# Narrow products for norms and key sums in a decoder layer's cross-attention, with ScalarE in written order

## The chip, the core and the metric

The kernel runs on one core of one Trainium2 chip. The metric is the device time of one execution in microseconds (us); lower is better. The core has TensorE (PE; its weight loads are listed as PEld), VectorE (DVE), ScalarE (ACT), GpSimd (POOL) and SyncE (SP, which here only issues DMAs), each with an instruction stream of its own, kept in step by semaphores.

## The reference

One decoder layer in float32 over x of shape (16, 128, 1024), three blocks with residuals:

```python
x = x + attn(layernorm(x), Wqkv, bqkv, Wo, bo)                 # 256 wide, one head
x = x + xattn(layernorm(x), ctx, ctx, Wq, Wk, Wv, Wo, bo, g)   # linear attention
x = x + ffn(layernorm(x), gate, up, down)                      # int4 weights, 1024 -> 2752 -> 1024
```

The second block takes each batch as 128 channels by 1024 positions. That is the one that the change is about:

```python
qh = softmax(Wq @ q, axis=-2) * SCALE   # 8 heads of 64, over the 64 channels of a head
kh = softmax(Wk @ k, axis=-1)           # over the 1024 positions
context = einsum('bhdn,bhen->bhde', kh, vh)
out = einsum('bhde,bhdn->bhen', context, qh) ; out = Wo @ out + bo
norm = maximum(sqrt(sum(out * out, axis=1)), 1e-12)   # over the 128 channels
return out / norm * g * sqrt(128)
```

Two sums over partitions occur in it: the denominators of the key softmax (per key channel, over positions) and the norm (per position, over the 128 channels).

## The kernel before

The program holds the layer twice: a fast form that takes exponentials without subtracting a maximum and raises a flag where a sum leaves a safe range, and a second form behind a branch, which runs only then. All that follows is about the fast form.

Stage 1 is self-attention over four groups of four batches, up to about 250 us. Beside it `early`, a generator made by `prepare`, dequantises int4 weights on VectorE (`pa`, then combinations `pc`) and stores them to DRAM as `wg`, `wu` and so on.

Stage 2 is cross-attention, from about 250 to 750 us, one batch after the other in the order of `batches`. The loop over a batch `b` alternates four times `key_unit` (for the next batch) and `query_unit` (for this one), and calls `tick()` after each, so a batch is eight units. Everything else is put in a list by `later(n, fn)`, "n ticks from now". TensorE, VectorE and SP are wrapped in `InOrder`, which keeps the instructions in the order in which the code emits them; ScalarE's and GpSimd's are placed by the scheduler.

- `key_unit`: a projection into a PSUM pair `kq` (two buffers), one exponential of 1024 columns on ScalarE into `ek`, and two units later a product with the context, `kx`. VectorE adds the four `ek` of a batch into `ksum`; at the end it adds its two halves.
- `mix`: four products of one column each with `ones` give the key sums (`mm<-ones,ksum`); then eight products of 64 output rows (`mm<-g_sb,kc`), which VectorE scales into `m_sb`.
- `query_unit`: a projection into `kq`, an exponential into `qe`, sums and reciprocals on VectorE, a multiplication on GpSimd, a transposing on VectorE (`kt`), and a trip through DRAM (`kd`, then `qs`, both issued by SP).
- `project_out(b, qs, st, when)`: four pieces of the output product at the ticks `when[0..3]`; ScalarE makes `y` and its square `sq` from each half. `norms`, at `when[4]`, multiplies `sq` by a 128 x 128 `ones`, so that all 128 output rows hold the same sums; ScalarE takes the logarithm and then exp(-0.5 ln) of [128, 1024], each with a load of its table. `scale`, `add`, `stats`, `row_shift` and `turned` follow one tick apart; `turned` normalises the row for stage 3 into `xn`, and `turn_rows` transposes it and stores it as `xt`.
- `rows` normalises the next batch's row on ScalarE (`xn`), after a small `row_shift` on VectorE.

`when` is written out by hand, for most batches:

```python
when = (14, 15, 16, 17, 18, 1, 1) if k < 13 else (13, 14, 15, 16, 17, 1, 1)
```

Stage 3 is the gated feed-forward block, by two levels of a seven-product scheme (`GATE`, `DOWN`). `one_block` multiplies the rows with weight tiles `w`, which `load_weights` brings from DRAM; `got` adds a PSUM bank and a kept copy into `sg` (gate) or `h` (up). `beside` runs between products; it ticks until the leftovers of stage 2 are done, calls `attention_done`, which makes the generator `rest` for the weights not yet prepared, and then takes steps of `rest`. VectorE and SP keep the written order here too. Stage 4, from about 1740 us, is the down projection.

Most helpers go through `InOrder`, so that their instructions all carry line 63 in the profile, and are told apart by their tiles.

Of the kernel before, what the change touches and what calls it, by code (L numbers as in the profile page):

```python
# [18 lines left out]
P = 128  # L19
# [47 lines left out]
def decoder_layer(  # L67
# [83 lines left out]
    def normalise_act(dst, src, b):  # L151
        nc.scalar.activation(
            dst, src, AF.Identity, bias=shift[:, b : b + 1], scale=rstd[:, b : b + 1]
        )
# [50 lines left out]
    def prepare(jobs, ahead, queue, vector=nc.vector, sync=nc.sync):  # L205
# [4 lines left out]
        stores = deque()  # L210

# [101 lines left out]
    give_pool = ExitStack()  # L313
    ag = give_pool.enter_context(tc.tile_pool(name="a_g", bufs=1, reuse_waits="tile"))
    with (
# [31 lines left out]
        def turn(b, xnT):  # L347

            xn = a2.tile([P, C], F32, name="xn")
            normalise(xn, X[b], b)  # L350
            nc.vector.tensor_copy(*turn_half(xn, xnT, b, 0))
            nc.scalar.copy(*turn_half(xn, xnT, b, 1))

        def first_rows(xnT):

            vector = InOrder(tc, nc.vector)
            halves = {}

            def stats(b):
                row_stats(b, vector)  # L360
                row_rstd(b, 1, vector)

            def rows(b):
                xn = a2.tile([P, C], F32, name="xn")
                row_shift(b, vector)
                normalise_act(xn, X[b], b)
                halves[b] = turn_half(xn, xnT, b, 0)
                nc.scalar.copy(*turn_half(xn, xnT, b, 1))

            def copy(b):  # L370
                vector.tensor_copy(*halves[b])

            for fn, b in (
                (stats, 0),
                (stats, 1),
                (rows, 0),
                (rows, 1),
                (stats, 2),
                (copy, 0),
                (copy, 1),  # L380
                (stats, 3),
                (rows, 2),
                (rows, 3),
                (copy, 2),
                (copy, 3),
            ):
                fn(b)
# [74 lines left out]
        def attend(atT, v):  # L462
            oT = ag.tile([P, 2, TB], F32, name="oT")
            for d in range(2):
                ps = aps.tile([P, BPT, S], F32, name="mm")
                for i in range(BPT):
                    nc.tensor.matmul(
                        ps[:, i, :], v[:, i, ts(d, P)], atT[:, i, :], start=True, stop=True
                    )
                nc.scalar.copy(oT[:, d, :], ps.rearrange("p i s -> p (i s)"))  # L470
            return oT
# [10 lines left out]
        for t in range(NT):  # L482
# [27 lines left out]
            v = a2.tile([P, BPT, DH], F32, name="v")  # L510
# [26 lines left out]
    sync = InOrder(tc, nc.sync)  # L537
# [66 lines left out]
    bek = unit_pool("b_ek", 3)  # L604
# [33 lines left out]
    if True:  # L638
# [17 lines left out]
        nc.sync.dma_start(wk_sb, xwk)  # L656
        ctxs = {batches[0]: load_ctx(batches[0])}
        wo_again = []
        for d in range(2):
            wo_again.append(bqs.tile([P, C], F32, name="wo_again", tag="qs"))  # L660
            nc.sync.dma_start(wo_again[d], wo[ts(d, P)])
        nc.sync.dma_start(wq_sb, xwq)
        nc.sync.dma_start(wv_sb, xwv.rearrange("(r p) s -> p r s", p=P))
        nc.sync.dma_start(xwo_sb, xwo.rearrange("(r p) o -> p r o", p=P))
        nc.sync.dma_start(xbo_sb, xbo)
        nc.sync.dma_start(gs_sb, xg)
        ctxs[batches[1]] = load_ctx(batches[1])
# [9 lines left out]
        def raise_flag():  # L677

            within = [bsm.tile([P, 1], F32, name=f"within{n}") for n in range(2)]

            def test(n):
                op, limit, holds = (
                    (ALU.max, LIMIT, ALU.is_le),
                    (ALU.min, 1 / LIMIT, ALU.is_ge),
                )[n]
                vector.tensor_reduce(within[n], sums, AX.X, op)
                vector.tensor_scalar(within[n], within[n], limit, None, holds)

            def count():
                ps = bps.tile([P, 1], F32, name="mm")  # L690
                for n in range(2):
                    tensor.matmul(ps, ones, within[n], start=(n == 0), stop=(n == 1))
                vector.tensor_copy(flag, ps[0:1])

            later(1, lambda: test(0))
            later(2, lambda: test(1))
            later(5, count)

        def mix_weights():

            D = DIM_HEAD
            for e in range(2):
                ps = bps.tile([P, 4, S], F32, name="mm")
                for r in range(4):
                    tensor.matmul(
                        ps[:, r, :],
                        wv_sb[ts(e, D), r, :],
                        xwo_sb[ts(e, D), r, :],
                        start=True,
                        stop=True,  # L710
                    )
                dst = g_sb.rearrange("p (r e) o -> p e r o", e=2)[:, e]
                nc.scalar.mul(dst, ps, D**-0.5)
# [15 lines left out]
        def key_unit(ctx, p, st):  # L729
# [14 lines left out]
            ek = bek.tile([P, 2, 512], F32, name="ek")  # L744
            nc.scalar.activation(ek, ps, AF.Exp)

            def use():
# [11 lines left out]
                if p == 1:  # L759
                    st["sum"] = bas.tile([P, 2, 512], F32, name="ksum")  # L760
# [3 lines left out]
                if p == 3:  # L764
                    t = st["sum"]
                    vector.tensor_tensor(t[:, 0], t[:, 0], t[:, 1], ALU.add)
                    st["kc"] = b1.tile([P, HIDDEN], F32, name="kc")
                    nc.scalar.copy(st["kc"], st["ps"])
                    later(4, lambda: mix(st))
# [3 lines left out]
        def mix(st):  # L773

            D = DIM_HEAD
            ks = bps.tile([P, 4], F32, name="mm")
            for r in range(4):
                tensor.matmul(
                    ks[:, r : r + 1], st["sum"][:, 0, ts(r, P)], ones[:, 0:1], start=True, stop=True
                )  # L780
            ksum = sums_tile(4, B * 8 * HEADS + 4 * st["b"], "ksum")
            krec = bsm.tile([P, 4], F32, name="krec")
            vector.tensor_copy(ksum, ks)
# [18 lines left out]
        def query_unit(b, pair, qs, wait):  # L802
# [9 lines left out]
            if plain:  # L812
                nc.scalar.activation(qe, heads, AF.Exp)  # L813
            else:
# [3 lines left out]
                nc.scalar.activation(qe, qe, AF.Exp)  # L818
# [31 lines left out]
        def turned(b):  # L850

            xn = b1.tile([P, 2 * JC, P], F32, name="xn3")
            for n in range(2):
# [3 lines left out]
                normalise_act(dst, rows, b)  # L857
# [8 lines left out]
        def project_out(b, qs, st, when):  # L866
            out, bank = {}, {}

            def piece(h, part):
                if h == part == 0:  # L870
                    out["y"] = b1.tile([P, C], F32, name="y")
                    out["sq"] = b1.tile([P, C], F32, name="sq")
                if part == 0:
                    bank[h] = bps.tile([P, 512], F32, name="mm")
                ps, y, sq = bank[h], out["y"], out["sq"]
# [10 lines left out]
                nc.scalar.activation(y[:, ts(h, 512)], ps, AF.Identity, bias=xbo_sb)  # L886
                nc.scalar.activation(sq[:, ts(h, 512)], ps, AF.Square, bias=xbo_sb)

            def norms():
                y, sq = out["y"], out["sq"]  # L890

                for h in range(2):
                    ps = bps.tile([P, 512], F32, name="mm")
                    tensor.matmul(ps, ones, sq[:, ts(h, 512)], start=True, stop=True)
                    nc.scalar.activation(sq[:, ts(h, 512)], ps, AF.Ln)
                nc.scalar.activation(sq, sq, AF.Exp, scale=-0.5)
                steps = (scale, add, stats, lambda: row_shift(b, vector), lambda: turned(b))
                for n, step in enumerate(steps):
                    later(when[5] + n * when[6], step)
# [16 lines left out]
        def rows(b):  # L916
            xn = b0.tile([P, C], F32, name="xn2", tag="xn2")
            row_shift(b, vector)
            normalise_act(xn, X[b], b)
            return xn  # L920

        T0 = {}

# [18 lines left out]

        xns = {batches[0]: rows(batches[0])}
# [10 lines left out]
        for k, b in enumerate(batches):  # L954
# [4 lines left out]
            if len(ahead) == 2:  # L959
                when = (14, 15, 16, 17, 18, 1, 1) if k < 13 else (13, 14, 15, 16, 17, 1, 1)  # L960
            elif ahead:
                when = (12, 13, 14, 15, 16, 1, 0)
            else:
                when = (10, 10, 11, 11, 12, 1, 1)
            project_out(b, qs, keys[b], when)
            if ahead:
                later(5, lambda n=ahead[0]: xns.update({n: rows(n)}))
            if len(ahead) == 2:
                later(2, lambda n=ahead[1]: ctxs.update({n: load_ctx(n, sync)}))
            for n in (5,) if k < 12 else ():  # L970
# [11 lines left out]
    give_pool.close()  # L982
# [57 lines left out]
    with ExitStack() as gs:  # L1040
# [4 lines left out]
        cw = pool("c_w", 5)  # L1045
# [4 lines left out]
        def attention_done():  # L1050
# [6 lines left out]
            rest = prepare(todo[MIDDLE:], 2, nc.sync, vector)  # L1057
# [28 lines left out]
        def load_weights(queue=nc.sync):  # L1086
            if to_load:
                wt = cw.tile([P, 2, 512], F32, name="w")
                todo = to_load.popleft()
                for n, (blk, mat, q) in enumerate(todo):  # L1090
# [480 lines left out]
        for n in range(AHEAD):  # L1571

            load_weights(nc.scalar if n == 0 else nc.sync)
# [5 lines left out]
        def beside(n, mat, q):  # L1579
# [19 lines left out]
            if rest is None or blk == 0:  # L1599
                return  # L1600
            if blk == RB:
# [3 lines left out]
            else:  # L1605
                more = mat == "g" and blk < 4
                steps = (1, 1 + (mat == "g"), 1, more, 1, 0, 0)[n % 7]
# [310 lines left out]
```

## Time and profile before

| | |
|---|---|
| time, three runs | 2221.77, 2221.79, 2223.6 us (median 2221.79) |
| the profiled execution | 2223.65 us, its span 2221.8 us |
| TensorE busy | 2191.3 us, 99% of the span |
| VectorE, ScalarE, GpSimd busy | 1559.9, 507.7, 562.6 us |
| DMA | 425.27 MB, mean 191 GB/s |
| granted TensorE clock over the span | 0.997 |

Times in the profile are counted from the span's start. A group of instructions is shown as line, engine, operation, output<-inputs, shapes and count, and then its busy time, the mean of one in ns, and the idle time of the engine before it with what ended it. A matrix product in float32 appears as two records. The ends of products are modelled, so that the start of the next one tells more than a duration.

### The profile page before, as it was taken

To read this page: it belongs to the slowest core of one execution; us is meant where nothing else is said; L and a number is where in the kernel's file an instruction comes from. 1 tells how busy PE (TensorE), PEld (TensorE's weight loads), DVE (VectorE), ACT (ScalarE), POOL (GpSimd) and SP (SyncE) were. 2 spreads that over 40 slices of the span, in tenths; PEclk is the share of its full clock that TensorE was granted. 3 is DMA by queue.
4 is the path that set the end of the run, shared out by engine and by line. 5 is a ranking of instruction groups with operands and counts; after the bars stand their busy time and mean duration, and the time that the engine had idled before them with its cause. 6 is when DMAs were issued, how large, how long until landed. Compare 5 with 4: busy or idle time off the path is not lost.

```text
span 2221.8 us, 24458 instructions
## 1 busy us (share of the span) xinstructions
PE 2191.3 (99%) x8500; PEld 1547.4 (70%) x8500; DVE 1559.9 (70%) x2119; ACT 507.7 (23%) x684; POOL 562.6 (25%) x442
## 2 busy tenths in 40 slices
PE   8999999999999998999999999999999999999998
PEld 7556555555555553444788588888887788888887
DVE  7897577888887647675799768787786645544462
ACT  2111235665556531111111111212121000000000
POOL 5453134333333300000344244444442000000000
PEclk9999999999999999999999999999999999999999
DMA  6435447777795758999434735464455965334631
GB/s 253 159 127 188 138 147 239 225 233 230 231 294 183 237 176 279 286 327 283 161 115 139 202 102 180 143 209 164 159 199 184 342 198 184 102 120 140 218 119 40
DMA packets 268725, 425.27 MB, mean 191 GB/s; under 512 B 28784, under 2 KB 130544, under 8 KB 268464
## 3 DMA queue, kind: packets, MB, share of 16 engines
q1 hardware_dynamic: 239584, 368.54, 52.3%
q0 software_dynamic: 10704, 35.92, 4.4%
q10 hardware_dynamic: 18304, 19.14, 2.7%
q8 instruction: 70, 1.15, 0.2%
q14 instruction: 63, 0.52, 0.1%
HBM read 265.62 MB, written 157.35 MB: 190 GB/s over the span
## 4 chain that ended last, share of the span: by engine, by line
PE 91%; DVE 5%; issue 2%; DMA 1%; SPq 0%; ACT 0%; POOL 0%; DVEq 0%; POOLq 0%; ACTq 0%
PE q L63 24%; PE po L1797 21%; PE p L63 13%; PE kq L63 10%; PE mm L63 8%; PE kx L63 5%; PE mm L397 4%; PE p L1166 2%; PE mm L412 2%; DVE pa L63 2%; PE mm L295 1%; DVE ti L63 1%; DVE C L63 1%; PE tr L344 1%; DVE pc L63 0%
## 5 line engine op out<-in xcount | busy, mean ns | idle before, releaser
L63 PE MATMUL q<-ti,li 128*128 128x256 f32 x1176 | 271.6, 380 | 3.6 <-ACT k L63 3.3
L63 PEld LDWEIGHTS q<-ti,li 128*128 128x128 f32 x1176 | 222.5, 190 | 37.7 <-POOL li L63 5.2
L63 POOL TENSOR_TENSOR li<-w 128x512 f32<-128x512 f32 x98 | 141.2, 1443 | 340.1 <-DMA w<-wu 293.5
L63 PE MATMUL p<-b,w 128*128 128x512 f32 x432 | 192.6, 598 | 6.4 <-DVE sg L63 6.4
L825 POOL TENSOR_TENSOR qe<-qe,qrec 128x1024 f32<-128x1024 f32 x64 | 148.1, 2314 | 180.1 <-DVE qrec L63 156.0
L63 ACT COPY k<-q 128x512 f32<-128x512 f32 x147 | 85.9, 584 | 464.9 <-PE q L63 464.9
L1797 PE MATMUL po<-wc,lc 128*128 128x256 f32 x840 | 183.4, 379 | 0.0
L1797 PEld LDWEIGHTS po<-wc,lc 128*128 128x128 f32 x840 | 159.6, 190 | 21.8
L63 PEld LDWEIGHTS p<-b,w 128*128 128x128 f32 x432 | 82.7, 192 | 110.9 <-issue 99.9
L63 PE MATMUL p<-T,w 128*128 128x512 f32 x304 | 134.7, 592 | 0.0
L1797 PE MATMUL po<-wq,lq 128*128 128x256 f32 x560 | 126.7, 379 | 0.4 <-issue 0.4
L63 PEld LDWEIGHTS mm<-qs,m_sb 128*128 128x128 f32 x512 | 97.3, 190 | 40.1 <-issue 29.7
L63 DVE STREAM_TRANSPOSE kt<-qe 128x1024 f32<-128x1024 f32 x64 | 79.4, 1241 | 64.5 <-POOL qe L825 62.3
L63 PE MATMUL kq<-wq_sb,xn 128*128 128x512 f32 x256 | 120.3, 593 | 1.6 <-ACT qe L813 1.6
L63 PE MATMUL kx<-ek,cxt 128*128 128x512 f32 x256 | 121.8, 598 | 0.0
L63 PE MATMUL mm<-qs,m_sb 128*128 128x256 f32 x512 | 120.8, 379 | 0.0
L63 PE MATMUL kq<-wk_sb,cx 128*128 128x512 f32 x256 | 120.1, 592 | 0.0
L1797 PEld LDWEIGHTS po<-wq,lq 128*128 128x128 f32 x560 | 106.0, 190 | 16.1 <-issue 1.3
L397 PE MATMUL mm<-xnT,wqkv_sb 128*128 128x512 f32 (+1 forms) x320 | 113.3, 510 | 0.0
L63 POOL TENSOR_TENSOR li<-w,li 128x512 f32<-128x512 f32 x49 | 66.2, 1352 | 180.1 <-PE q L63 179.6
L63 DVE TENSOR_TENSOR pa<-pa,sz 128x1024 f32<-128x1024 int32 x86 | 108.8, 1265 | 2.4
L63 PEld LDWEIGHTS p<-T,w 128*128 128x128 f32 x304 | 57.8, 190 | 72.7 <-issue 72.2
(193 smaller groups left out, 3755.6 us busy)
## 6 DMA issues: line engine op xcount, KB each, us to landing
w<-wu SPq DMA_DIRECT2D x140, 256.0 KB, 3.4
lq<-h SPq DMA_DIRECT2D x140, 256.0 KB, 4.4
w<-wg SPq DMA_DIRECT2D x138, 256.0 KB, 2.8
kd<-kt SPq DMA_DIRECT2D x64, 512.0 KB, 3.6
qs<-kd SPq DMA_DIRECT2D x256, 128.0 KB, 3.3
h<-hc SPq DMA_DIRECT2D x80, 256.0 KB, 2.8
wq<-wd SPq DMA_DIRECT2D x70, 256.0 KB, 5.2
h<-h SPq DMA_DIRECT2D x60, 256.0 KB, 2.1
```

The source lines that it names most:

```text
L63: return lambda *args, **kw: self._tc.keep_in_program_order(fn(*args, **kw))
L295: tensor.matmul(ps, oT[:, d, ts(b % BPT, S)], wo_d[d][:, ts(h, 512)], start=(d == 0), stop=(d == 1),)
L344: nc.tensor.transpose(tr[:, j, :], xn[:, ts(4 * h + j, P)], ident)
L397: nc.tensor.matmul(ps[:, tokens], wqkv_sb[:, f, c, :], xnT[:, c, tokens], start=(c == 0), stop=(c == CC - 1),)
L412: nc.tensor.matmul(ps, xnT[:, c, ts(i, S)], wqkv_sb[:, 4:6, c, :], start=(c == 0), stop=(c == CC - 1),)
L825: nc.gpsimd.tensor_tensor(qe, qe, rec.unsqueeze(2).to_broadcast(wide), ALU.mult)
L1166: tensor.matmul(ps, wt[:, j, :], T[q][:, :, j], start=(first == q and j == 0), stop=(q in (2, 3, 4) and j == JC - 1), skip_group_check=True,)
L1797: nc.tensor.matmul(bank[:, i, :], l[:, ts(i, S)], w,  start=(start and c == 0 and i % 2 == 0), stop=(stop and c == len(pairs) - 1), skip_g ...
```

## The change

1. `norms`, for the batches k = 0 to 12: four products with `ones[:, :32]`, each for 256 positions, write to partitions 0, 32, 64 and 96 of one [128, 256] tile. The logarithm and the exponential are 256 columns wide. The four rows go to a small DRAM tensor `rn_flat` by ScalarE's DMA queue, and one unit later the same queue loads them back, broadcast to all 128 partitions of `sq`. The last three batches keep the direct form (`direct_norm`).
2. `mix`: the key sums come from eight products of 32 output rows and 128 columns, accumulated over the two halves of `ksum`, and a transposing on VectorE; the addition of the halves goes away.
3. ScalarE is wrapped in `InOrder` in stage 2. `row_shift` is emitted two units before `rows`; the steps after `norms` are spaced 3, 4, 5, 7 and 9 ticks from it, and two pieces of the output product come one tick earlier. The squares are made before `y`.
4. The tiles `oT`, `xn`, `v` of stage 1, `ek` and `ksum` of stage 2 and `w` of stage 3 share one pool of five buffers; the first weight tile of stage 3 is loaded a batch ahead, on SP. The loads at the start of stage 2 go through the ordered SP.
5. The first step of `rest` only issues its loads, and the steps beside the products of stage 3 are dealt out anew.

```diff
-        def project_out(b, qs, st, when):
+        def project_out(b, qs, st, when, direct_norm):
...
-                for h in range(2):
-                    ps = bps.tile([P, 512], F32, name="mm")
-                    tensor.matmul(ps, ones, sq[:, ts(h, 512)], start=True, stop=True)
-                    nc.scalar.activation(sq[:, ts(h, 512)], ps, AF.Ln)
-                nc.scalar.activation(sq, sq, AF.Exp, scale=-0.5)
+                if direct_norm:
...
+                else:
+                    ps = bps.tile([P, 2 * P], F32, name="mm")
+                    for c in range(4):
+                        tensor.matmul(
+                            ps[ts(c, Q)], ones[:, :Q], sq[:, ts(c, 2 * P)], start=True, stop=True
+                        )
+                    rn = sq[:, ds(0, 2 * P)]
+                    scalar.activation(rn, ps, AF.Ln)
+                    scalar.activation(rn, rn, AF.Exp, scale=-0.5)
+                    flat = dram.tile([4, 2 * P], F32, name="rn_flat", tag="rn_flat", bufs=2)
+                    scalar.dma_start(flat, rn[0:P:Q])
+                    row = flat.rearrange("c n -> (c n)").partition_broadcast(P)
+                    later(1, lambda: scalar.dma_start(sq, row))
...
-            if len(ahead) == 2:
-                when = (14, 15, 16, 17, 18, 1, 1) if k < 13 else (13, 14, 15, 16, 17, 1, 1)
...
+            if k < 12:
+                when = (14, 15, 15, 16, 18, (3, 4, 5, 7, 9))
+            elif k == 12:
+                when = (14, 15, 15, 16, 17, (3, 4, 5, 6, 8))
...
-            for r in range(4):
-                tensor.matmul(
-                    ks[:, r : r + 1], st["sum"][:, 0, ts(r, P)], ones[:, 0:1], start=True, stop=True
-                )
...
+            ks = bps.tile([P, 4, Q], F32, name="mm")
+            parts = st["sum"].rearrange("p i (r c q) -> p i c r q", r=4, c=4)
+            for i in range(2):
+                for c in range(4):
+                    tensor.matmul(
+                        ks[ts(c, Q)], ones[:, :Q], parts[:, i, c], start=(i == 0), stop=(i == 1)
+                    )
+            kt = st["sum"][:, 0, ds(0, P)]
+            vector.transpose(kt, ks.rearrange("p r q -> p (r q)"))
...
-            rest = prepare(todo[MIDDLE:], 2, nc.sync, vector)
+            rest = prepare(todo[MIDDLE:], 2, nc.sync, vector, loads_first=True)
...
-                more = mat == "g" and blk < 4
-                steps = (1, 1 + (mat == "g"), 1, more, 1, 0, 0)[n % 7]
+                steps = (1, 1 + (n == 1 < blk), 1, n == 3 and blk < 4, 1, 0, 0)[n % 7]
```

## The prediction

> **What bounds the kernel now.** I read the page first, then the list of waits for TensorE, TensorE's groups with shapes kept apart, the table of stages, and the timelines round three places.
>
> ```profile
> span 2221.8 us, 24458 instructions
> PE 2191.3 (99%) x8500; PEld 1547.4 (70%) x8500; DVE 1559.9 (70%) x2119; ACT 507.7 (23%) x684; POOL 562.6 (25%) x442
> ```
>
> TensorE is idle for 30.5 us of the span. So a gain has two sources only: less time in its products, or less of that idle time. The waits say which engine ends the latter:
>
> ```profile
> PE tr L344 <- ACT xn L152: 9.2, 1, 9.2
> PE p L63 <- DVE sg L63: 6.4, 2, 6.1
> PE kq L63 <- ACT qe L813: 1.6, 1, 1.6
> ```
>
> The first is the start of the program, which the change leaves. The groups that it touches, with two for comparison (count, busy us, mean ns):
>
> ```profile
> L63 PE MATMUL mm<-sq,ones 128*128 128x512 f32 x64 | 30.2, 592 | 0.0
> L63 PE MATMUL mm<-ones,ksum 128*128 128x1 f32 x128 | 15.2, 240 | 0.0
> L63 PE MATMUL mm<-g_sb,kc 128*64 128x128 f32 x256 | 17.5, 279 | 0.0
> L427 PE MATMUL mm<-qkT 128*128 128x128 f32 x64 | 7.8, 275 | 0.0
> ```
>
> Two records stand for one float32 product (64 records of `sq`, 32 products in the code). The mean is a latency; the busy time divided by the count is the spacing. A 128-column product on the whole array takes 7.8 / 64 = 0.122 us a record; one with 64 output rows (`g_sb,kc`, "128*64") takes 17.5 / 256 = 0.068. Two products on the two halves of the array therefore run side by side. Inside one batch:
>
> ```profile
> 342.08 0.95 PE L63 MATMUL mm<-ones,ksum 128*128 128x1 f32 x8
> 342.96 1.09 PE L63 MATMUL mm<-g_sb,kc 128*64 128x128 f32 x16
> 343.98 0.70 PE L63 MATMUL kx<-ek,cxt 128*128 128x512 f32 x1
> ```
>
> The eight one-column records take 0.88 us to the next start, bound by their weight loads. The sixteen half-width ones take 1.02 us. In the chain of waits a stretch of eight 512-column records is 3.43 us, so 0.43 each and 0.107 for 128 columns; eight pairs would be 0.86 us. They cost 0.16 more, and the `kx` behind takes 0.70 instead of the usual 0.59, 0.11 more. About 0.3 us is what I charge for going to narrow products and back.
>
> ```profile
> 290.00:740.00 450.00, 450.00 (x1563) 255.53 (x1562) 369.71 (x456) 257.35 (x293) 165.94 (x113) 1.00 0.74 227
> 842.00:848.00 6.00, 5.15 (x7) 2.27 (x8) 5.90 (x11) 1.26 (x2) 0.00 (x0) 0.56 0.96 341
> ```
>
> Columns: length, then busy time of PE, PEld, DVE, ACT, POOL, then clock, DMA share, GB/s. In the cross-attention stage TensorE never idles; VectorE is 82% busy, ScalarE 57%, DMA 74%. A batch takes 31.2 us. The second row is the only place after the start with a lowered clock, behind this wait:
>
> ```profile
> 835.12 0.76 DVE L63 TENSOR_SCALAR pa<-raw 128x512 int32<-128x512 int32 x2 [5.66 <-DMA wu<-pa]
> 838.32 0.68 DVE L63 TENSOR_TENSOR sg<-p,k 128x512 f32<-128x512 f32 x1
> 842.85 7.63 PE L63 MATMUL p<-b,w 128*128 128x512 f32 x12 [6.06 <-DVE sg L63]
> ```
>
> VectorE sat 5.66 us before a third dequantised pair until the store of the first had left its buffer. The addition for the first gate of feed-forward block 1 stood behind it, and TensorE ran out of free banks. Its next 12 products took 7.63 us instead of 12 x 0.43 + 0.17 = 5.33: 2.3 us to the clock. The place costs 8.4 us.
>
> **Part by part.**
>
> *Norms.* Thirteen of sixteen batches replace two products (four records of 512 columns, 1.72 us) by four of 32 output rows and 256 columns: eight records of 0.215. The trace has no product of 32 rows. Upper bound of the cost: side by side in pairs but in chain (a product's second record beside the next one's first), five steps of 0.215 and 0.3, 1.4 us; lower bound: four abreast with free switching, 0.43. The nearest row is `g_sb,kc`, whose records pair fully, so I take four abreast with its switching price: 0.43 + 0.3 = 0.73. Saved: 0.99 x 13 = 12.9 us; between 4.2 and 16.8.
>
> *Key sums.* Sixteen batches replace 0.88 us by sixteen records of 128 columns and 32 rows, next to `g_sb,kc`, which already pays the way out and back. Four abreast: 4 x 0.107 + 0.3 = 0.73; in pairs 8 x 0.107 + 0.3 = 1.16; four abreast with free switching 0.43. I take 0.73 by the same rule: 0.15 x 16 = 2.4 us saved; between -4.5 and +7.2. VectorE loses a 512-wide addition and gains a 128-wide transpose, off the path.
>
> [...]
>
> *ScalarE.* Per batch two logarithms of 512 columns and an exponential of 1024 (1.08 + 1.06 us in the timeline) become 256-wide ones, and two DMA issues (0.41 each, from 0.82 for two weight loads issued on this queue) come in. Busy time falls by about 0.7 us a batch and is not the bound. The row load is new: it waits on ScalarE's queue until the 4 KB row has landed in DRAM, with the next query's exponential behind it. From the end of the norm product: logarithm, table load, exponential and issue take 2.6 us; ahead of the row load stand a key exponential and two halves of `xn` (1.0 + 1.7), which ends 6.3 us after that product. So a landing of up to 3.7 us is hidden. TensorE asks for that query bank again only after the mix, a `kx` and a key product, about 2.6 us later still. Tiny loads issued by SP took 2.0 us to land (`gs_sb`), the 512 KB `kd` stores 2.6 to 6.9. I cost it at nothing; uncovered, each microsecond over 6.3 costs 13.
>
> *Row load to its users.* 512 KB, 3.9 to 6.6 us by `x_all` and `cxt`, so at `sq` 11 to 14 us after the norm product. VectorE's scaling is placed three units on, at about 11; it may wait up to 3 us, against 1.85 now (24.1 us in 13 waits for `sq`). VectorE has 4 to 5 idle us a batch. The bytes, 13 x 0.5 MB, lift the DMA share from 0.74 to about 0.8.
>
> *Moves.* Pieces 3 and 4 of the output product come one unit earlier, 11 us after their `qs` loads are issued (those land in 3.3). The turned rows, their stores on SP and `x_all` on POOL's queue come four units later; nothing reads them before the next stage. ScalarE's squares come first and must wait for the scaled `y` of the batch before: still one unit apart. The first weights move from ScalarE's queue to SP a batch earlier, and are not late today. Nothing for these.
>
> *End of the stage.* The 1.64 us wait at 746.4 is for an exponential behind the norms of batch 13. Now two `xn` halves (1.66 us) stand before it: +1.7 us.
>
> *Feed-forward block 1.* Loads of the remaining preparation get a step of their own, and the order on VectorE puts the first two gate additions before the third pair. The store then has a product (3.44 us) more to land, so I take 8.0 of the 8.4 us; bounds 0 and 8.4, since DMA is 96% busy there.
>
> Sum: -12.9 - 2.4 + 1.7 - 8.0 = -21.6 us on a span of 2221.8. The profiled execution took 2223.65, 1.9 above it, and was near the slowest of the three runs; their median is 2221.79. Subtracted from that: 2200 us.
>
> **Rivals.**
>
> *Only pairs, in chain.* Norms save 4.2, key sums lose 4.5; with the other terms -6.0: 2216 us. Speaking for it: two records share a column group, and only halves are proved. Against: the half-width records pair without loss.
>
> *The gate wait stays.* It is DMA that ends it, and the stage that follows runs at 0.90 of DMA. Then 2208 us.
>
> *The row blocks ScalarE.* The landing of the row takes long behind other transfers, and TensorE waits for a query bank in each of 13 batches. It decides the sign once the landing exceeds 6.3 us by 21.6 / 13 = 1.7, so 8.0 us; at 9.5 it is 3.2 x 13 = 41.6 us, 2242 us. Against it: the largest `kd` store, 128 times the bytes, took 6.9.
>
> **How the numbers follow.** My forecast has 0.55 (2195 to 2206), pairs 0.18, the staying wait 0.16, the blocked ScalarE 0.11. Low end: norms 16.8, sums 7.2, gate 8.4, less 1.7 gives 2191. High end: the pairs' 2216. Above that lie the last rival and a little of the second. 0.2%, 4.4 us, is about what a measurement of this kernel can tell from no change. Faster by more: forecast, wait and most of the pairs, 0.84; within: 0.06; slower: 0.10.
>
> **What would show it.** The `sq` group of 32 rows: 104 records, 0.06 us each if four abreast, 0.13 if in chain. The `ksum` group: 0.73 us to `g_sb,kc`. TensorE's waits: no `sg` of 6 us, the clock at 1.00 in block 1, one `qe` wait of about 3.3 us. The batch at 30.0 us instead of 31.2. If new waits of TensorE for `qe` or `ek` appear in every batch, the forecast is wrong by the row; if none appear and the batch is still 31, by the narrow products.

## The result and the profile after

The changed kernel took 2259.59 us (median of four runs, 2252.26 to 2264.06), the kernel before 2222.59 us on the same chip: a ratio of 1.0163, with a 95% interval of 1.0135 to 1.0191. It is 37 us slower, where I had forecast 22 us faster.

The page's head shows TensorE idle for 65 us of the span, where it was 30.5:

```profile
span 2258.5 us, 24828 instructions
PE 2193.5 (97%) x8680; PEld 1536.0 (68%) x8680; DVE 1579.0 (70%) x2119; ACT 492.5 (22%) x673; POOL 554.4 (25%) x442
```

Now the products that the change is named for, in TensorE's groups with shapes kept apart (count, busy us, mean ns):

```profile
L63 PE MATMUL mm<-ksum,ones 128*32 128x128 f32 x256 | 10.3, 279 | 0.0
L63 PE MATMUL mm<-sq,ones 128*32 128x256 f32 x104 | 8.3, 391 | 0.0
```

A norm record costs 8.3 / 104 = 0.08 us, not the 0.13 of products in chain: more than two products do run side by side. The timeline of TensorE in one batch gives the whole price, switching included:

```profile
344.79 0.64 PE L63 MATMUL mm<-sq,ones 128*32 128x256 f32 x8
345.36 1.98 PE L63 MATMUL kx<-ek,cxt 128*128 128x512 f32 x4
...
350.70 0.65 PE L63 MATMUL mm<-ksum,ones 128*32 128x128 f32 x16
351.28 1.09 PE L63 MATMUL mm<-g_sb,kc 128*64 128x128 f32 x16
```

The norms take 0.57 us to the next start (1.72 before), the key sums 0.58 (0.88 before). Eight norm records in pairs would be four steps of 0.215, 0.86 us, so four products do run abreast. The product ahead of each group takes 0.1 us longer than usual to the next start (1.81 instead of 1.72), and so does the `kx` behind the norms. So the named gain is there. The waits of TensorE show where more than that was lost (in all, times, longest):

```profile
PE mm L63 <- DMA qs<-kd: 19.7, 12, 4.1
PE kx L63 <- ACT ek L63: 8.5, 1, 8.5
PE p L63 <- DVE sg L63: 4.6, 2, 3.8
PE q L63 <- DVE ti L63: 3.4, 6, 2.0
PE kq L63 <- ACT qe L63: 3.4, 2, 3.1
PE p L1215 <- DVE h L63: 2.8, 1, 2.8
```

The two largest did not exist before, and the gate's one wait of 6.1 us has become two of 3.8 and 2.8. Most of those over 2 us cost more than their length, since the granted clock falls to 0.50 behind them: from 200 to 2200 us it does so in eight stretches, 41 us in all. Two rows of the table of stages, of the whole stage and of 4 us behind a `qs` wait of 3.4 us (length, busy us of the engines, clock, DMA share, GB/s):

```profile
290.00:740.00 450.00, 432.66 (x1659) 232.09 (x1658) 366.82 (x440) 229.55 (x267) 159.19 (x110) 0.98 0.71 228
653.00:657.00 4.00, 4.00 (x10) 2.77 (x10) 2.64 (x4) 0.68 (x2) 0.74 (x2) 0.50 1.02 274
```

The DMA share of the stage fell from 0.74 to 0.71: no shortage of bandwidth on average. The 8.5 us stand at the start of the stage, in the timeline of VectorE, ScalarE and TensorE:

```profile
259.15 0.15 DVE L63 TENSOR_SCALAR gs_sb<-gs_sb 128x1 f32<-128x1 f32 x1 [8.76 <-DMA gs_sb<-in_xg]
...
259.50 1.24 ACT L63 ACTIVATE xn<-X,shift,rstd 128x1024 f32<-128x1024 f32 x1 [9.13 <-DVE shift L63]
260.65 1.92 ACT L63 ACTIVATE ek<-kq 128x1024 f32<-128x1024 f32 x2
261.70 2.93 PE L63 MATMUL kx<-ek,cxt 128*128 128x512 f32 x3 [8.52 <-ACT ek L63]
```

VectorE waits for a tiny load, its `shift` stands behind that, and ScalarE, now in the order of the code, has `xn` ahead of the first `ek`. Before, ScalarE made `ek` first, and the same wait of VectorE hurt nobody:

```profile
252.27 1.02 ACT L745 ACTIVATE ek<-kq 128x1024 f32<-128x1024 f32 x1 [1.14 <-DMA wo_again<-in_wo]
...
259.03 0.15 DVE L63 TENSOR_SCALAR gs_sb<-gs_sb 128x1 f32<-128x1 f32 x1 [7.88 <-DMA gs_sb<-in_xg]
...
259.38 1.24 ACT L152 ACTIVATE xn<-X,shift,rstd 128x1024 f32<-128x1024 f32 x1 [4.37 <-DVE shift L63]
```

The `qs` waits have their reason in SP's queue. Its waits in the stage, two lines from before and four from after:

```profile
SPq L63 <- DMA kd<-kt: 178.8, 45, 7.3
SPq L63 <- DVE kt L63: 87.2, 46, 22.4
```

```profile
SPq L63 <- DMA kd<-kt: 138.0, 46, 6.1
SPq L63 <- DMA rn_flat<-sq: 48.5, 13, 6.7
SPq L63 <- DMA sq<-rn_flat: 36.2, 11, 4.4
SPq L63 <- DVE kt L63: 21.4, 2, 21.0
```

and in one batch, SP's and ScalarE's DMA issues:

```profile
349.37 1.08 ACTq L63 DMA_DIRECT2D rn_flat<-sq  x1
...
352.86 0.36 ACTq L63 DMA_DIRECT2D sq<-rn_flat  x1
352.90 0.33 SPq L63 DMA_DIRECT2D cxt<-in_cxt  x1
353.33 6.82 SPq L63 DMA_DIRECT2D qs<-kd  x4
```

SP issues neither of the row's DMAs and reads neither `rn_flat` nor `sq`, yet it waits 84.7 us for the two to land. Each DMA instruction in the trace carries the number of the semaphore on which its landing is recorded. Those of SP and ScalarE share eight (100, 102 to 106, 108 and 109); GpSimd's use another eight (111 to 118). In the trace of the kernel before, each of the 1550 DMAs of SP and ScalarE that took a number over was issued after the last landing of the one that had it; in the changed kernel's, the 591 on the three numbers with every landing recorded show no exception. Here `cxt` takes 106, that of the row's store, and goes 0.04 us behind the row load, which waits for the same store. The second of the four `qs` loads takes 109, that of the row load, whose last landing is at 358.15 us, and goes at 358.17 us, 4.8 us behind the first; the four took 6.82 us to issue, where 1.8 is usual. Before, SP waited 87.2 us for `kt`: it was ahead of VectorE. Now that is 21.4, so it runs late, and the `qs` loads with it.

### The profile page after: what moved, and what is told of

It reads as the page before. It is cut to its first block, busy times and chain, and to the rows that moved or that the text cites. A ratio compares the mean times of both kernels' runs of the same rounds, so it can differ in the third digit from the quotient of the medians.

```text
span 2258.5 us, 24828 instructions
## 1 busy us (share of the span) xinstructions
PE 2193.5 (97%) x8680; PEld 1536.0 (68%) x8680; DVE 1579.0 (70%) x2119; ACT 492.5 (22%) x673; POOL 554.4 (25%) x442
## 4 chain that ended last, share of the span: by engine, by line
PE 76%; DVE 9%; DMA 8%; issue 3%; ACT 2%; SPq 1%; POOL 0%; ACTq 0%; DVEq 0%; POOLq 0%
PE po L1847 21%; PE q L63 20%; PE p L63 12%; PE kq L63 5%; PE mm L63 5%; PE mm L412 4%; PE kx L63 3%; DMA kd<-kt 3%; DVE pa L63 2%; PE p L1215 2%; PE mm L427 2%; DVE ti L63 2%; DMA qs<-kd 2%; DMA sq<-rn_flat 1%; DVE C L63 1%
## 5 line engine op out<-in xcount | busy, mean ns | idle before, releaser
L63 PE MATMUL mm<-qs,m_sb 128*128 128x256 f32 x512 | 125.8, 395 | 19.7 <-DMA qs<-kd 19.7
L63 PEld LDWEIGHTS mm<-qs,m_sb 128*128 128x128 f32 x512 | 100.0, 197 | 59.6 <-issue 43.1
L63 PE MATMUL kx<-ek,cxt 128*128 128x512 f32 x256 | 127.2, 621 | 8.5 <-ACT ek L63 8.5
L1847 PEld LDWEIGHTS po<-wq,lq 128*128 128x128 f32 x560 | 106.3, 190 | 15.8 <-issue 1.4
```

The source lines that it names most:

```text
L63: return lambda *args, **kw: self._tc.keep_in_program_order(fn(*args, **kw))
L1847: nc.tensor.matmul(bank[:, i, :], l[:, ts(i, S)], w,  start=(start and c == 0 and i % 2 == 0), stop=(stop and c == len(pairs) - 1), skip_g ...
```

## The experiments

Theory: the products pay as forecast, and two queues lose more, ScalarE's at the start of the stage and SP's in every batch. Rivals: pieces 3 and 4 of the output product, taken one unit earlier, are late by themselves; or the 13 x 512 KB of row loads slow all transfers.

**The first normalised rows behind the second key exponential.**

```diff
-        xns = {batches[0]: rows(batches[0])}
+        xns = {}
...
             key_unit(ctxs[batches[0]], oc, keys[batches[0]])
+            if oc == 1:
+                xns[batches[0]] = rows(batches[0])
```

> Only the place of the first normalised rows in ScalarE's program order changes: behind the second key exponential, not ahead of the first. Theory (ScalarE's order at the start of the cross-attention stage costs 8.5 us of waiting and 2.4 us of half clock): the kx wait for ek of 8.5 us is gone, TensorE's other waits stay, 2248 us, 11 less than the changed kernel. Rival (the start is bound by the loads, and the wait only gets another name): a wait of 8 us for another tile in the same place, 2259 us.

Measured: 2246.35 us, ratio 1.0101 (1.0083 to 1.0119), 13.2 us less than the changed kernel. The `kx` wait is gone, `ek` starts at 252.13 us as before the change, and the `qs` waits stay at 20.5 us. ScalarE's place for one instruction cost about 13 us (11 were expected; the changed kernel's own runs spread over 12).

**All norms wide again, so no row.**

```diff
-            project_out(b, qs, keys[b], when, k > 12)
+            project_out(b, qs, keys[b], when, True)
```

> All 16 batches take the old norm products of 128 rows, so there is no row, no store and no load of it; key sums, piece times and ScalarE's order stay as changed. Theory (the row's two DMAs hold up SP's queue, and with it the qs loads): the qs waits (19.7 us) and the slow clock behind them (about 10 us) go, the norms cost 15 us more, 2244 us. Rival (the pieces that come one unit earlier are late by themselves): the qs waits stay, 2274 us.

Measured: 2244.55 us, ratio 1.0100 (1.0083 to 1.0117), as the theory had it. The norms of two batches stand 31.02 us apart in every undisturbed batch, and the waits of TensorE and of SP's queue say:

```profile
PE mm L63 <- DMA qs<-kd: 2.6, 1, 2.6
```

```profile
SPq L63 <- DMA kd<-kt: 137.9, 45, 6.8
SPq L63 <- DVE kt L63: 113.5, 43, 21.0
SPq L1140 <- DVE ksum L63: 14.5, 1, 14.5
```

With the pieces still early, one `qs` wait is left: the early pieces are not late by themselves. SP is ahead of VectorE again. Its third line is one that I had passed over: a feed-forward weight load stood 14.5 us in SP's queue (8.3 in the changed kernel) until the last `ksum` freed its buffer.

**The row's two DMAs issued by GpSimd.**

```diff
-                    scalar.dma_start(flat, rn[0:P:Q])
+                    nc.gpsimd.dma_start(flat, rn[0:P:Q])
...
-                    later(1, lambda: scalar.dma_start(sq, row))
+                    later(1, lambda: nc.gpsimd.dma_start(sq, row))
```

> The row's store and load are issued by GpSimd instead of ScalarE; bytes, times and order of all else stay. Theory (SP is held up because its DMAs and ScalarE's take turns in one set of completion semaphores, which GpSimd's are not part of): SP's waits for rn_flat and sq go, the qs waits shrink from 19.7 us to under 5, 2232 us. Rival 1 (13 x 512 KB more on the DMA engines make all loads slow): qs waits stay near 20 us, 2259 us. Rival 2 (GpSimd, which multiplies the queries, stands still while the row lands): qs waits stay or grow, with waits of GpSimd for rn_flat, 2259 us or more.

Measured: 2249.41 us, ratio 1.0114 (1.0097 to 1.0131), 10.2 us less than the changed kernel. The waits of SP for `rn_flat` and `sq` are gone, with the same bytes moved, so these 10 us were the queue's and not the bandwidth's. Eight of the first nine batches take 30.1 us, as forecast. But four `qs` waits remain, 14.4 us in all, one of 8.1 us in the last batches, so my figure of 5, and the 2232 us, were too good. The same line of SP as above stands there (`SPq L1140 <- DVE ksum`, 14.5 us).

Neither rival is ruled out for the rest. GpSimd waited 16.1 us, in 7 times, for the row's store to land, and VectorE 15.7 us, in 6, for the row. And the wait of 3.4 us at 645 us stands in the slice of the page (618 to 674 us) where DMA moved 276 GB/s, against 234 to 257 in the five slices before it; without the row it was 271 there, and TensorE did not wait from 290 to 740 us. Which of these made the `qs` late is not shown.

The 26 DMAs given to another issuer saved 10.2 us, and ScalarE, which issued them in the changed kernel, had waited for the row only 1.8 us in all there: the saving is what no longer stood behind them on SP.

**Pieces 3 and 4 at their old units, the row on ScalarE.**

```diff
-                when = (14, 15, 15, 16, 18, (3, 4, 5, 7, 9))
+                when = (14, 15, 16, 17, 18, (3, 4, 5, 7, 9))
```

> Pieces 3 and 4 of the output product go back to their old units (16 and 17), with the row's DMAs where the change put them. A unit is 3.75 us, and the longest qs wait is 4.2. If lateness of SP and earliness of the pieces add up, the qs waits fall under 4 us in all, 2231 us. If SP's lateness alone decides (it grows with what is given back), waits of 10 us or more stay, 2250 us.

Measured: 2264.37 us, ratio 1.0188 (1.0171 to 1.0205), no gain. The `qs` waits are 21.5 us in 16 times, none over 3.5. The rival holds, even beyond its number: the 3.75 us given to the loads are lost again. That the `qs` buffers come free a unit later too may be the reason; I did not test it.

**Three mends at once:** the first normalised rows behind the second key exponential, the row on GpSimd, and the first weight loads of the feed-forward stage kept in SP's written order (the third is shown).

```diff
-            load_weights()
+            load_weights(sync)
```

> The changed kernel with three mends at once: the first normalised rows behind the second key exponential, the row's DMAs issued by GpSimd, and the first four feed-forward weight loads of SP kept in program order, behind the last qs loads. Theory (the late qs in the last batches, 8.1 us in one wait with GpSimd issuing the row, come from these weight loads: two of them stand in SP's queue ahead of qs loads and wait for the last key sum to free their buffer): that wait and the slow clock behind it go, 10 us; with the 13 us of the start 2226 us. Rival (those qs are late through GpSimd's row, not through the weights): the wait of 8 us stays, 2236 us.

Measured: 2229.95 us, ratio 1.0037 (1.0026 to 1.0048). With 13.2 us for the start taken off the run with the row on GpSimd, 2236.2, the weights' place was worth 6 us, if the two add up, and not the 10 expected: the wait of 8.1 us became one of 4.4. The first gate product starts at 749.05 us (751.89 before the change, 781.28 after it). So the kernel is 2.8 us ahead at that point, of the 16 that the products bring, and falls back behind it.

**The mends with the preparation steps dealt out as before.**

```diff
-            rest = prepare(todo[MIDDLE:], 2, nc.sync, vector, loads_first=True)
+            rest = prepare(todo[MIDDLE:], 2, nc.sync, vector)
...
-            if blk == 0:
-                steps = 1
...
-                steps = (1, 1 + (n == 1 < blk), 1, n == 3 and blk < 4, 1, 0, 0)[n % 7]
+                more = mat == "g" and blk < 4
+                steps = (1, 1 + (mat == "g"), 1, more, 1, 0, 0)[n % 7]
```

> The three mends, and the preparation beside the first feed-forward blocks dealt out as before the change (no step of its own for the loads, none in block 0). Theory (the new dealing only moved VectorE's wait for a store: sg 4.1 us and 1.7 of slow clock, about 960 us): that wait goes, the old one of 6 us with 2.3 of slow clock in block 1 comes back, and the time is within 4 us of the kernel with three mends. Rival (the new dealing does take the old wait away, and what shows now has another cause): the old wait comes on top, 8 us slower.

Measured: 2227.45 us, ratio 1.0023 (1.0013 to 1.0033), 2.5 us less than with the new dealing, which is not clear of the spread of the two. The `sg` wait of 5.5 us at 945 us is gone, and one of 4.1 us stands at 846.5, where the old one was. The theory holds: the new dealing moved a wait for a store from block 1 to a later addition and gained nothing that can be measured.

**The kernel before, with narrow key sums alone** (against the kernel before; the transposing of `ks` and what reads it as in the change).

```diff
-                    t = st["sum"]
-                    vector.tensor_tensor(t[:, 0], t[:, 0], t[:, 1], ALU.add)
...
-                    later(4, lambda: mix(st))
+                    later(3 if st["b"] == batches[0] else 4, lambda: mix(st))
...
-            ks = bps.tile([P, 4], F32, name="mm")
+            ks = bps.tile([P, 4, Q], F32, name="mm")
...
+                    tensor.matmul(
+                        ks[ts(c, Q)], ones[:, :Q], parts[:, i, c], start=(i == 0), stop=(i == 1)
+                    )
```

> The kernel before with the narrow key sums alone (and the mix of the first batch one unit earlier, which their longer use of the sum needs). With wide norms and narrow sums a batch took 31.0 us instead of 31.2; 16 times 0.2 is 3.3, so 2219.5 us if nothing else is behind it. If the sums' gain was lost elsewhere in the changed kernel, for example to the transpose on VectorE, no less than 2222.

Measured: 2225.62 us, ratio 1.0013 (1.0004 to 1.0023): slower by 2.9 us, not faster by 3.3. The batch is 31.02 us instead of 31.23, so the sums bring their 0.2 us. They lose it at two places: `kx` waits once for `ek` (1.5 us, ScalarE standing before `xn`), and the first gate product, ready earlier, waits 3.2 us for its weights. The two are 4.7 of the 6.1 us between forecast and result; the rest is not accounted for.

**The kernel before, with narrow sums and norms,** the row on GpSimd, the steps behind it two units later (on top of the last edit).

```diff
+                    nc.gpsimd.dma_start(flat, rn[0:P:Q])
+                    row = flat.rearrange("c n -> (c n)").partition_broadcast(P)
+                    later(1, lambda: nc.gpsimd.dma_start(sq, row))
...
-                when = (14, 15, 16, 17, 18, 1, 1) if k < 13 else (13, 14, 15, 16, 17, 1, 1)
+                when = (14, 15, 16, 17, 18, 3, 1) if k < 13 else (13, 14, 15, 16, 17, 1, 1)
```

> The kernel before with the narrow key sums and the narrow norms alone: the row's DMAs on GpSimd, the three VectorE steps behind them two units later; ScalarE's order, the shared buffers, the piece times and the feed-forward loads stay as before. Theory (the products bring 1.1 us a batch, and all that was lost came with the row's place on ScalarE's queue and with what was moved beside it): a batch of 30.1 us, 2208 us. Rival (the row's way costs what the product brings even there, by late qs, late scaling or GpSimd's order): 2219 us or more.

Measured: 2231.84 us, ratio 1.0048 (1.0032 to 1.0065). The rival's side in the time, though not by the causes that it named: a batch takes 30.1 to 33.2 us, with waits of TensorE for `sq` (11.3 us in 8 times). ScalarE, placed by the scheduler, stood before `xn`, for 4.81 us in the batch at 366 us, with the squares behind it.

**Late pieces with the three mends and the old dealing.**

```diff
-                when = (14, 15, 15, 16, 18, (3, 4, 5, 7, 9))
+                when = (14, 15, 16, 17, 18, (3, 4, 5, 7, 9))
...
-                when = (14, 15, 15, 16, 17, (3, 4, 5, 6, 8))
+                when = (14, 15, 16, 17, 18, (2, 3, 4, 5, 7))
```

> The kernel with three mends and the old dealing of preparation steps, and now pieces 3 and 4 of the output product back at their old units. Theory (with the row off SP's set of semaphores, the two qs waits left, 2.9 and 2.8 us with slow clock behind them, are the price of taking the pieces a unit earlier): they go, about 8 us, 2219 us. Rival (as in the run with the old pieces alone, what is given in time is taken by a later load): 2227 us, qs waits of 5 us or more in all.

Measured: 2231.24 us, ratio 1.0035 (1.0022 to 1.0047). The `qs` waits fell from 5.4 to 3.9 us only, and waits for `qe` (3.1 to 7.2 us) and `sq` (1.8 to 5.4) grew. The rival holds again.

**The kernel before with both narrow products and three more parts of the change:** the square first, shifts two units ahead, the steps behind the norms at the change's units, but ScalarE left to the scheduler.

```diff
-                nc.scalar.activation(y[:, ts(h, 512)], ps, AF.Identity, bias=xbo_sb)
                 nc.scalar.activation(sq[:, ts(h, 512)], ps, AF.Square, bias=xbo_sb)
+                nc.scalar.activation(y[:, ts(h, 512)], ps, AF.Identity, bias=xbo_sb)
...
+                late = (3, 4, 5, 7, 9) if not direct_norm else [when[5] + n * when[6] for n in range(5)]
...
-            row_shift(b, vector)
...
+                later(3, lambda n=ahead[0]: row_shift(n, vector))
```

> The kernel before with the narrow key sums and norms, the row on GpSimd, and three things more from the change: the square before the copy of y, the shift of the normalised rows made two units ahead of them, and the VectorE steps behind the norms at the change's units. ScalarE is not in program order; shared buffers, first weights and feed-forward steps stay as before. Theory (the 11.3 us of waits for sq with the narrow products put into the kernel before come from ScalarE standing before xn, 4.8 us for a shift, ahead of the squares): those waits go, a batch takes 30.1 us, 2215 us. Rival (the scheduler puts ScalarE's work so that another wait takes their place): 2225 us or more.

Measured: 2289.92 us, ratio 1.0295 (1.0277 to 1.0312), the worst of all. TensorE's and ScalarE's waits:

```profile
PE mm L63 <- ACT sq L891: 46.5, 13, 5.4
```

```profile
ACT xn L152 <- DVE shift L63: 93.9, 15, 8.3
```

The wait that I had named, ScalarE before `xn`, is the right one, but it grew. In the batch that norms at 374 us ScalarE waits 8.27 us before `xn`, against 4.81 in the run with the two narrow products: the scheduler left `xn` where it was, ahead of the squares, and the `shift` that it needs now comes a unit later. In 13 batches TensorE waits for a square behind it. Here the change's program order pays: with it, and the row off SP's set (three mends), TensorE waits for a square once, 3.9 us in the feed-forward stage.

**Batch 12 moved,** on top of the mends and the old dealing.

```diff
-                when = (14, 15, 15, 16, 17, (3, 4, 5, 6, 8))
+                when = (14, 15, 16, 17, 18, (2, 3, 4, 5, 6))
```

> The kernel with three mends and the old dealing of steps, and batch 12 alone with its pieces 3 and 4 and its norms one unit later and its turned rows one unit earlier. Theory (the qs wait of 2.8 us at 727 us comes from that batch's early pieces, and the qe wait of 3.1 at 742 from its turned rows, which stand on ScalarE ahead of that exponential): the first goes, the second falls to about 1.6, and with the slow clock behind both 2221 us. Rival (each is replaced by another wait, as with the old pieces for all batches): 2227 us or more.

Measured: 2221.36 us, ratio 0.9992 (0.9983 to 1.0001), the best of all, level with the kernel before. The number is the theory's, the way is not: `qs` waits (5.8 us) and the `qe` wait (3.6) stayed, the waits for `h` and `sq` of the feed-forward stage went, and a new one came:

```profile
PE p L1217 <- DMA w<-wg: 5.9, 1, 5.9
```

**Narrow sums in the kernel before, their two losses mended** (on top of the run with the sums alone).

```diff
-            row_shift(b, vector)
...
+                later(3, lambda n=ahead[0]: row_shift(n, vector))
...
-            load_weights(nc.scalar if n == 0 else nc.sync)
+            load_weights(nc.gpsimd if n == 0 else nc.sync)
```

> The kernel before with the narrow key sums alone, the shift of the normalised rows made two units ahead, and the first feed-forward weights loaded by GpSimd's queue instead of ScalarE's. Theory (the narrow sums bring 0.2 us a batch, and what took it back are the one wait of 1.5 us for ek behind a late shift and the one of 3.2 us for weights at the start of the feed-forward stage): both go, 2220 us. Rival (the weights wait for the buffers that they share, not for a queue): a wait of 3 us for w stays, 2224 us.

Measured: 2236.92 us, ratio 1.0060 (1.0046 to 1.0074). Both waits grew: `ek` 2.1 us, the weights 7.8. GpSimd issues them at 757.93 us, ScalarE did at 749.70. Neither text has that: the queue did matter, and the loads went out later on GpSimd's.

**The second weight tile loaded earlier,** on top of batch 12 moved.

```diff
-        def first_weights():
+        def first_weights(at=0):
...
-                sync.dma_start(wt[:, n], wprep[0, "g"][n])
+                sync.dma_start(wt[:, n], wprep[0, "g"][at + n])
...
+            if k == B - 1:
+                later(2, lambda: first_weights(2))
...
-                    loaded.append((early_w.pop(), len(todo)))
+                    loaded.append((early_w.pop(0), len(todo)))
```

> The kernel before this one in the list (three mends, old dealing of steps, batch 12 moved) with the second tile of feed-forward weights loaded by SP in the last batch, after its second unit, instead of behind all of the stage's qs loads. Theory (the wait of 5.9 us for w comes from the second weights' place in SP's order alone; nothing else in the stage is short): it goes, no new qs wait comes, 2215 us, faster than the kernel before the change. Rival (a place between the qs loads makes those late again, by the buffer that the weights take from the last keys): 2221 us or more.

Measured: 2226.12 us, ratio 1.0010 (1.0001 to 1.0019). The wait for weights went, the `qs` waits stayed at 5.6 us, and a wait for `sq` of 5.0 us and one for `sg` of 4.5 came; those for `qe` grew from 3.6 to 5.1. Neither text has that. TensorE's order in the first feed-forward block is the scheduler's, and it seems that a small shift re-deals which of the last batch's products come late there. No version that I ran beats the kernel before beyond what can be measured.

## Why the prediction was wrong

**Right: the two sums.** Forecast were 0.99 us a batch for the norms and 0.15 for the key sums, by four products abreast and 0.3 us of switching. The distance between the norms of two undisturbed batches is 31.23 us before, 31.02 with narrow sums, 30.07 with both: 0.95 and 0.21. Times 13 and 16 that is 12.4 + 3.4 = 15.8 us against 15.3. The rival of pairs in chain is out.

**Wrong: "I cost it at nothing", for the row's store and load.** I followed them on ScalarE's own queue, and there the sum held: in the batch shown the row landed 3.5 us after its store was issued, inside the 3.7 that I had called hidden, and ScalarE waited for it 1.8 us in all. I never asked what other queue had to pass them. Taking the row away, with the norms made wide, gave 15.0 us although the norms cost 12.4 more, so the row's DMAs cost some 27 us. Moving them to GpSimd gave 10.2 of these back: that much is shown to be SP's queue. The 17 that stayed are `qs` waits with the slow clock behind them, of which the weights below are a part; the rest is open. My rival of the row had the right sign and the wrong engine: ScalarE was not blocked, SP was. What I held against it was wrong as well: the largest `kd` store of the stage before took 8.6 us to land, not 6.9, and its size is no guide. The 4 KB store of the batch shown took 3.5 us; before, the 512 KB `kd` stores took 3.6 as a median and the 256 KB `lq<-h` loads 4.4.

**Wrong: ScalarE's program order, which I had not costed as a change of order.** I sized ScalarE's busy time per batch and took the start of the stage as it was. One `xn` ahead of the first `ek` cost 13.2 us. The rows were at hand: before, `xn` came at 259.38 us, seven behind the first `ek`, and waited for a `shift` behind a tiny load.

**Wrong: nothing for the weights.** I looked at the first tile alone, which moves to SP a batch earlier, and costed its move with "Nothing for these". What cost time were the loads of the tiles behind it. They went through SP before, too, but the shared pool now gives them a buffer that the last key sum holds, and the scheduler had put two of them ahead of `qs` loads. About 6 us, from the run with three mends.

**Mis-sized: the gate.** Forecast was a gain of 8.0 us. From the first gate product to the first inner product (`q<-ti`) it took 318.9 us against 315.3 before, a loss of 3.6. The wait for a store went to another addition, and an `h` wait came, behind the last batch's norms. My lower bound, no gain, was still too good.

**Mis-sized: the end of the stage.** The `qe` wait is 3.1 us, as forecast (1.6 + 1.7 = 3.3). But the four records behind it lose another 1.4 us to the clock (3.42 us instead of 1.98). I had not charged that. Of the 3.10 us of idle time 2.62 lie in one step of the clock's record (the last section), and a slow stretch of 3.41 us starts at 774.12 us. With the old dealing the wait is 3.07 us and the four records behind it take 3.78; that the loss is chance was not shown.

Together: 13.2 + 27.4 + 6 + 11.6 + 1.4 = 59.6, less 0.5 for the better products, so 59.1 against 59.4 us between forecast and median. The parts are differences between runs, the changed kernel's own runs spread over 12 us, and the parts overlap in the last batches (the 27.4 holds some of the 6), so that the sum closes this well is luck. Seen from TensorE, its idle time grew by 34.5 us of the span's 36.7, and from 200 to 2200 us its clock was at half for 41 us instead of 6.8. The early pieces, costed at nothing, cost nothing that I could find.

What stays open: why the feed-forward stage re-deals its waits with each small shift of the last batches. I did not put TensorE's first block into written order to see.

## What to carry to other kernels

When a DMA is added to one queue, list the queues whose DMAs carry the same semaphore numbers in the trace, and ask what stands behind it in each; here SP stood 84.7 us in all behind the 26 row DMAs of ScalarE, until those whose numbers it took next had landed. When an engine goes from scheduled to written order, walk through the first instructions of each stage in the new order, with what each waits for. And a wait taken away at a stage's end is worth only the distance to the next one: several edits here removed the wait that they aimed at and met another of about its size.

## What I had not expected of the hardware

TensorE's clock fell behind shorter waits than I had reckoned with, and not behind all of them. In the changed kernel, behind a `qs` wait of 2.7 us the eight records took 3.38 us instead of 1.89, and behind one of 3.4 us they took 3.75 and the clock stood at 0.50 for 4 us; behind one of 2.44 us they took 2.87, and behind one of 2.39 us 1.97:

```profile
725.36 2.87 PE L63 MATMUL mm<-qs,m_sb 128*128 128x256 f32 x8 [2.44 <-DMA qs<-kd]
...
760.96 1.97 PE L63 MATMUL mm<-qs,m_sb 128*128 128x256 f32 x8 [2.39 <-DMA qs<-kd]
```

With the row on GpSimd, even a wait of 3.38 us was harmless:

```profile
645.29 1.97 PE L63 MATMUL mm<-qs,m_sb 128*128 128x256 f32 x8 [3.38 <-DMA qs<-kd]
```

The clock's records in the traces before and after show where the waits fell. From 200 to 2150 us the changed kernel has eight slow stretches, of 3.41, 6.83 or 10.24 us, and their starts lie whole multiples of 3.41 us apart: 255.30, 555.67 and 651.24 us, for example, 88 and 28 steps. In steps counted from these starts, by the modelled ends of TensorE's products, eight of the 561 steps at full clock hold 2.11 to 3.24 us of idle time, and a slow stretch starts at the end of each; the others hold at most 1.90, and no slow stretch starts behind them. The kernel before has one step of 3.41 us of idle time, with a slow stretch of 6.83 us behind it, and none over 1.50 besides. The wait of 2.44 us lies in one step; that of 2.39 is split, 1.90 and 0.49. So in these two traces it counted where a wait fell; whether the 3.38 us of the other run were split, I did not show. A slow stretch of 3.41 us at a clock of 0.50 takes 1.7 us of work away, by an estimate from these two numbers.
